# Attention gated by a feed-forward layer: one transpose for both query tiles of a short-reach head

## The chip, the cores and the metric

The kernel runs on one core of one Trainium2 chip. The metric is device time in microseconds (us), taken as the median of several executions. One execution was also recorded by the profiler.

## The reference

The input x has 1024 rows of 512 numbers. After a layer normalisation, two branches are computed from it and joined:

```
xn = layernorm(x)
s  = attention(xn)        # 32 query heads, 8 key/value heads, head size 128
g  = silu(ffn(xn))        # 4-bit weights with scales and zeros, 1792 wide
out = x + s * g
```

The attention is causal with ALiBi, and q and k are normalised per head:

```
scores = q @ k.T / sqrt(128)
bias   = slope[head] * (key - query)  if key <= query else -1e30
attn   = softmax(scores + bias)       # over the keys
s      = concat(attn @ v) @ Wo.T
slope[head] = 0.8409 ** (head + 1)
```

The slopes are steep for the first heads, so that distant keys get weights that vanish. The queries and keys decide whether that holds; the kernel compares this at run time and has a second path without the shortcut.

## The kernel before

**Stages.** The feed-forward branch comes first, then the projections to q, k and v (12 of them, each over 8 row tiles of 128), then the attention with its output projection. The first attention steps are already laid between the tiles of the last projection.

**Units and steps.** The queries are cut into 4 blocks of 256 (`qb` = 0 to 3), each of two query tiles of 128 (`qt` = 0, 1). A unit `u` is one head in one block: `g` is the key/value head, `hh` the head among its 4, so head = 4g + hh. There are 128 units, hence 256 steps `n`, one for each (u, qt). For g = 0 the blocks come in the order 3, 2, 1, 0, for the next ones 2, 3, 0, 1; the 4 heads of a block follow each other. A hand-written order puts the work of several units into each step:

- `scores` at step n: three matmuls for each 512 columns (high and low half of fp16 pairs) into one of two PSUM buffers `s`.
- `biased` and `exponentials` one step later: DVE adds the bias and takes the row's least value (L1073), ACT exponentiates (L1079) into `pf`.
- `split_hi` three steps later: ACT writes the high half of p as fp16 into `p16` (L1098). `split_lo` four steps later: DVE writes the low half beside it (L1106), and SP issues the DMA that transposes the pair of halves from `p16` into `pT` (L1114).
- `values` nine and ten steps later (`AV_LAG`): PE multiplies the transposed p with `vT` into PSUM `o`. Half of the key tiles go into each of the two steps. Key tiles that both query tiles see are one matmul of 256 columns; a tile at either edge of the band has 128 columns.
- `heads_hi`, `heads_lo`, `out_proj` (tile `m`) and `accumulate` follow.

**Reach.** `REACH[head]` is the number of key tiles that a query tile looks back over, its own included: 2 for heads 0 to 2, 3 for heads 3 to 6, 4 for heads 7 to 9, 5 for head 10, 6 for head 11, and 8 (all) from head 12 on. `lowest(u, qt)` is the first key tile of a query tile. Where the reach binds, the two query tiles of a unit see equally many key tiles, the second one tile later than the first.

**Buffers.** `p16` is a ring of 5 slots of 16 blocks of 128x128 fp16 each (`P16_BUFS`). A query tile takes one slot, however little of it it uses. Only in block qb = 0 do both query tiles share a slot: there one DMA transposes both (L1109), with 8 blocks, of which POOL sets some to zero (L1094). `pT` comes from two rings of two slots each, named `wide` and `pT`, taken by turns; it lies as (key tile, half, query), so that the two query tiles of a key tile are 256 neighbouring columns:

```
pT[u] = rings["wide" if u % 4 < 2 else "pT"].take(F16, NT, 2, QB)
sp.dma_start_transpose(
    pT[u][:, k0 : k0 + nk, :, qt * P : qt * P + P]..., h16...)
```

**Queues.** All DMAs are issued by SP in program order: the transposes of p, and between them the loads of keys (L981), values (L985), queries (L993) and of Wo (`load_wo`, L1020, tile `wl`). In a step the loads of keys, values and queries come ahead of `split_lo`; those of Wo end the step.

Of the kernel before, what the change touches and what calls it, by code (L numbers as in the profile page):

```python
# [13 lines left out]
F16 = mybir.dt.float16  # L14
# [8 lines left out]
P = 128  # L23
# [8 lines left out]
NT = S // P  # L32
# [4 lines left out]
NQT = QB // P  # L37
# [76 lines left out]
def attention_gated_by_ffn_kernel(ctx, tc, x, gu_w, gu_z, gu_s, dn_w, dn_z, dn_s, wq, wkv, wo, qnw, knw, out):  # L114
    nc = tc.nc
    ve, se, ge, te, sp = nc.vector, nc.scalar, nc.gpsimd, nc.tensor, nc.sync
# [4 lines left out]
    rings = {}  # L121
# [4 lines left out]
    def ps2():  # L126
        return rings["s"].take(F32, 2, 512)

    def ps1(tag):
        return rings[tag].take(F32, 512)  # L130
# [22 lines left out]
    def mm3(ps, lhs, rhs, first, last):  # L153
        (lh, ll), (rh, rl) = lhs, rhs
        te.matmul(ps, lhsT=lh, rhs=rh, start=first, stop=False)  # L155
        te.matmul(ps, lhsT=lh, rhs=rl, start=False, stop=False)  # L156
        te.matmul(ps, lhsT=ll, rhs=rh, start=False, stop=last)  # L157
# [697 lines left out]
    for it in range(NI):  # L855
        for tb in range(2):
# [14 lines left out]
            for i in range(4):  # L871
                c = slice(i * P, i * P + P)
# [102 lines left out]
    units = [(g, qb, hh) for g, qbs in blocks for hh in range(NH) for qb in qbs]  # L975
    kT, vT, qT, woh, wol = {}, {}, {}, {}, {}
    trel, pT, oT, wor = {}, {}, {}, {}
# [64 lines left out]
    s_ps, pf, rows16, p16, av_ps, op_ps = {}, {}, {}, {}, {}, {}  # L1042

    def lowest(u, qt):

        g, qb, hh = units[u]
        return max(0, NQT * qb + qt + 1 - REACH[g * NH + hh]) if near[0] else 0

    def scores(u, qt):
        g, qb, hh = units[u]  # L1050
        k0 = lowest(u, qt)
        w = (NQT * qb + qt + 1 - k0) * P
        ps = ps2().rearrange("p a c -> p (a c)")
        q = qT[g, qb][:, qt]
        for c0 in range(0, w, 512):
            c1 = min(w, c0 + 512)
            kt = kT[g][:, k0 + c0 // P : k0 + c1 // P]
            mm3(ps[:, c0:c1], (q[:, 0, hh, :], q[:, 1, hh, :]), (kt[:, :, 0, :], kt[:, :, 1, :]), True, True)
        s_ps[u, qt] = ps[:, :w]
# [22 lines left out]
    def split_hi(u, qt):  # L1082
        least, total, inverse, scale = rows16[u]
        if qt == 0:
            ve.reciprocal(inverse, total)
            se.activation(scale, inverse, AF.Copy, scale=P_SCALE)
        nk = pf[u, qt].shape[1]
        if units[u][1]:
            p16[u, qt] = rings["p16"].take(F16, NT, 2, P)[:, :nk]
        elif qt == 0:  # L1090

            both = rings["p16"].take(F16, NT, 2, P)
            both = both.rearrange("p t a k -> p (t a k)")[:, : 4 * NQT * P].rearrange("p (t a i k) -> p t a i k", t=2, a=2, i=NQT)
            ge.memset(both[:, 1, :, 0, :], 0.0)  # L1094
            for i in range(NQT):
                p16[u, i] = both[:, : i + 1, :, i, :]
            p16[u] = both
        se.activation(p16[u, qt][:, :, 0, :], pf[u, qt], AF.Copy, scale=scale[:, qt : qt + 1])  # L1098

    def split_lo(u, qt):  # L1100
        p, h16 = pf.pop((u, qt)), p16.pop((u, qt))
        nk, k0 = p.shape[1], lowest(u, qt)
        if qt == 0:
            pT[u] = rings["wide" if u % 4 < 2 else "pT"].take(F16, NT, 2, QB)
        hi, lo, scale = h16[:, :, 0, :], h16[:, :, 1, :], rows16[u][3][:, qt : qt + 1]
        ve.scalar_tensor_tensor(lo, p, scale, hi, ALU.mult, ALU.subtract)  # L1106
        if u in p16:
            if qt == NQT - 1:
                sp.dma_start_transpose(  # L1109
                    pT[u][:, :NQT].rearrange("p t a (i q) -> p (t a i) q", i=NQT),  # L1110
                    p16.pop(u).rearrange("p t a i k -> p (t a i k)"),
                )
            return
        sp.dma_start_transpose(  # L1114
            pT[u][:, k0 : k0 + nk, :, qt * P : qt * P + P].rearrange("p t a q -> p (t a) q"), h16.rearrange("p t a k -> p (t a k)")
        )

    def values(u, part, between):
        g, qb, hh = units[u]
        if part == 0:  # L1120
            av_ps[u] = ps1("o")[:, :QB]
        ps = av_ps[u]
        k0, k1 = lowest(u, 0), lowest(u, 1)
        kts = [*range(k1, NQT * qb + 2), *range(k0, k1)]
        half = len(kts) // 2
        mine = kts[half:] if part else kts[:half]
        for kt in mine:
            if kt == mine[-1]:
                between()
            c0 = max(0, kt - NQT * qb) * P  # L1130
            c1 = P if kt < k1 else QB
            mm3(
                ps[:, c0:c1],
                (vT[g][:, kt, 0, :], vT[g][:, kt, 1, :]),
                (pT[u][:, kt, 0, c0:c1], pT[u][:, kt, 1, c0:c1]),
                kt == kts[0],
                kt == kts[-1],
            )
# [87 lines left out]
    def early_tile(c):  # L1226

        if c % 2 == 0:
            scores(*at(c // 2))
        for stage, lag in ((biased, 1), (exponentials, 2), (split_hi, 5), (split_lo, 6)):  # L1230
            if (c - lag) >= 0 and (c - lag) % 2 == 0:
                advance(stage, (c - lag) // 2)
# [8 lines left out]
    def step(n):  # L1241
        nonlocal last_ps
        if n < nn:
            u, qt = order[n]
            g, qb, hh = units[u]
            for due in q_at.get(n, ()):
                if due[0] < HKV - 1:
                    load_queries(*due)
            for t, due in LAST_QUERIES.items():
                if due == n:  # L1250
                    last_queries(t)
            if g + 1 < HKV:
                if n % (NB * BS) == KEYS_STEP:
                    relative(g + 1)
                    load_keys(g + 1)
                elif n % (NB * BS) == VALUES_STEP:
                    load_values(g + 1)
            scores(u, qt)
# [6 lines left out]
        for stage, lag in ((biased, 1), (exponentials, 1), (split_hi, NQT + 1), (split_lo, NQT + 2)):  # L1265
            advance(stage, n - lag)
            if stage is biased and ended is not None and units[ended][:2] != final:
                heads_lo(ended)
# [15 lines left out]
        if at(n - AV_LAG):  # L1284
            values(*at(n - AV_LAG), project)
        else:
            project()
# [60 lines left out]
    def everything():  # L1348

        if at(BRANCH - 1 - AV_LAG)[1] == 0:  # L1350
            values(at(BRANCH - 1 - AV_LAG)[0], 1, lambda: None)
        near[0], clock[0] = False, NT * len(projections) - NT
        for c in (kT, vT, qT, woh, wol, pT, oT, wor, s_ps, pf, rows16, p16, av_ps, op_ps):
            c.clear()
        for stage in stages:
            stages[stage] = 0
        relative(0)
        load_keys(0)
        for qb in blocks[0][1]:
            load_queries(0, qb)  # L1360
        load_values(0)
        for n in range(nn + AV_LAG + 1):
            step(n)
# [71 lines left out]
```

## Time and profile before

| | |
|---|---|
| median of 3 runs | 1003.09 us (1000.63 to 1004.23) |
| the profiled execution: time, span | 998.27 us, 996.5 us |
| PE busy | 945.7 us (95%) |
| DVE, ACT, POOL busy | 845.1 (85%), 762.0 (76%), 424.0 us (43%) |
| mean granted TensorE clock | 0.994 |
| DMA queue q1, share of 16 engines | 85.5% |
| transposes of p (L1114 and L1109) | 224 |
| attention steps | from about 442 us to the end |

PE is the TensorE's matmuls, DVE the VectorE, ACT the ScalarE, POOL the GpSimd, SP the SyncE. The line numbers are those of the kernel before. A number in square brackets after an instruction in a timeline is the idle time of its engine just before it, with what ended it. In a table of windows each line gives the stretch, its length, and then the busy time of each engine with its number of instructions. For a DMA issue, the view by line gives the shortest, median and longest time that SP spent on the issue, and in a line of its own the time from the issue to the landing.

### The profile page before, as it was taken

The page shows a single profiled execution, that of the slowest core. Times are in us where ns is not written, and L with a number is a line of the kernel's source. Part 1 is how long each engine was busy: PE and PEld are TensorE (multiplying, and loading weights), DVE is VectorE, ACT ScalarE, POOL GpSimd, SP SyncE. Part 2 cuts the span into 40 slices and gives each one's busy share as a digit, 9 for nine tenths or more (in the row PEclk, how much of TensorE's full clock was granted, in tenths as well). Part 3 has the DMA queues.
Part 4 walks back from the last instruction along what each step waited for, and adds up shares of the span by engine and source line. Part 5 has one row for each costly group of instructions (what it writes and reads, how often), then busy time and mean ns, then how long its engine had stood idle before and what let it go on. Part 6 is the DMA issues. An engine that isn't in the chain of part 4 may idle for free.

```text
span 996.5 us, 17926 instructions
## 1 busy us (share of the span) xinstructions
PE 945.7 (95%) x5595; PEld 550.7 (55%) x5595; DVE 845.1 (85%) x1769; ACT 762.0 (76%) x2161; POOL 424.0 (43%) x437
## 2 busy tenths in 40 slices
PE   7899999999999999999789999999999999989995
PEld 5344467864444444444556565675676666655562
DVE  7898998826988888886789989989989989979985
ACT  5777755678878778788878887878878978867861
POOL 1578864314666565656344231232222313234332
PEclk9999999999999999999999999999999999999999
DMA  7033249734798998997898998998999999999994
GB/s 241 27 118 125 97 125 301 266 127 122 170 255 221 220 259 197 249 256 211 167 205 178 207 209 177 232 203 181 233 202 177 224 191 203 195 231 206 212 207 115
DMA packets 413545, 192.79 MB, mean 193 GB/s; under 512 B 360003, under 2 KB 370559, under 8 KB 413439
## 3 DMA queue, kind: packets, MB, share of 16 engines
q1 hardware_dynamic: 413438, 191.55, 85.5%
q8 instruction: 46, 0.75, 0.3%
q14 instruction: 61, 0.49, 0.2%
HBM read 76.27 MB, written 27.27 MB: 104 GB/s over the span
## 4 chain that ended last, share of the span: by engine, by line
PE 73%; DVE 10%; DMA 8%; ACT 4%; issue 4%; POOL 1%; SPq 0%; DVEq 0%; POOLq 0%; ACTq 0%
PE o L155 8%; PE o L157 8%; PE o L156 8%; PE m L156 8%; PE m L157 8%; PE m L155 8%; PE gu_ps L334 6%; DMA wide<-p 4%; PE s L157 4%; PE s L155 4%; PE s L156 4%; DMA pT<-p 2%; DVE p L1106 2%; PE dn_ps L155 1%; PE dn_ps L157 1%
## 5 line engine op out<-in xcount | busy, mean ns | idle before, releaser
L1106 DVE SCALAR_TENSOR_TENSOR p<-pf,row,p 128x256 f16<-128x256 f32 (+7 forms) x256 | 204.1, 797 | 18.2 <-ACT p L1098 16.0
L1073 DVE CUSTOM_DVE_ANT_0 pf<-s,trel,cs 128x256 f32<-128x256 f32 (+7 forms) x256 | 185.8, 726 | 27.0 <-PE s L157 26.2
L1098 ACT ACTIVATE p<-pf,row 128x256 f16<-128x256 f32 (+7 forms) x256 | 179.3, 701 | 11.4 <-DMA wide<-p 3.2
L1079 ACT ACTIVATE pf<-pf,row 128x384 f32<-128x384 f32 (+7 forms) x160 | 123.2, 770 | 22.2 <-DVE row L1073 20.4
L155 PE MATMUL s<-kT,qT 128*128 128x512 f16 (+3 forms) x344 | 110.1, 320 | 4.5 <-DVE leasts L1073 2.7
L156 PE MATMUL s<-kT,qT 128*128 128x512 f16 (+3 forms) x344 | 110.2, 320 | 0.0
L157 PE MATMUL s<-kT,qT 128*128 128x512 f16 (+3 forms) x344 | 109.0, 320 | 0.0
L724 POOL TENSOR_TENSOR f<-f,inv 128x512 f32<-128x512 f32 (+1 forms) x96 | 99.4, 1056 | 1.3
L1023 POOL TENSOR_SCALAR wl<-wl,rvs 128x512 f32<-128x512 f32 x32 | 52.8, 1651 | 100.2 <-DMA wl<-in_wo 96.5
L1142 ACT ACTIVATE wh<-o 128x256 f16<-128x256 f32 x128 | 47.6, 372 | 60.8 <-PE o L157 60.5
L157 PE MATMUL m<-v,wh 128*128 128x512 f16 x248 | 94.0, 379 | 0.0
L155 PE MATMUL m<-v,wh 128*128 128x512 f16 x248 | 94.0, 379 | 0.0
L155 PEld LDWEIGHTS <-vT 128*128 128x128 f16 x574 | 56.3, 98 | 64.2 <-issue 11.5
L155 PE MATMUL o<-pT,vT 128*128 128x256 f16 (+1 forms) x292 | 75.4, 259 | 12.9 <-DMA pT<-p 10.1
L155 PE MATMUL o<-wide,vT 128*128 128x256 f16 (+1 forms) x282 | 72.9, 259 | 7.5 <-DMA wide<-p 5.6
L156 PEld LDWEIGHTS <-vT 128*128 128x128 f16 x574 | 56.3, 98 | 36.8
L156 PE MATMUL o<-pT,vT 128*128 128x256 f16 (+1 forms) x292 | 75.3, 258 | 0.0
L157 PE MATMUL o<-pT,vT 128*128 128x256 f16 (+1 forms) x292 | 75.0, 258 | 0.0
L155 PE MATMUL m<-wh,xth 128*128 128x512 f16 x192 | 72.8, 379 | 1.2 <-ACT h L898 1.2
L156 PE MATMUL o<-wide,vT 128*128 128x256 f16 (+1 forms) x282 | 72.9, 259 | 0.0
L157 PE MATMUL m<-wh,xtl 128*128 128x512 f16 x192 | 72.8, 379 | 0.0
L156 PE MATMUL m<-wl,xth 128*128 128x512 f16 x192 | 72.8, 379 | 0.0
(213 smaller groups left out, 2583.4 us busy)
## 6 DMA issues: line engine op xcount, KB each, us to landing
qd<-tr SPq DMA_DIRECT2D x48, 256.0 KB, 3.3
qT<-qd SPq DMA_DIRECT2D x24, 512.0 KB, 4.4
wide<-in_wq SPq DMA_DIRECT2D x32, 256.0 KB, 3.9
wo_sq<-in_wo SPq DMA_DIRECT2D x8, 1024.0 KB, 7.8
wl<-in_wo SPq DMA_DIRECT2D x32, 256.0 KB, 3.3
gui<-in_gu_w SPq DMA_DIRECT2D x13, 512.0 KB, 3.6
wide<-in_wkv SPq DMA_DIRECT2D x16, 256.0 KB, 3.7
vd<-v SPq DMA_DIRECT2D x8, 512.0 KB, 4.1
```

The lines of the kernel that those rows point to most:

```text
L155: te.matmul(ps, lhsT=lh, rhs=rh, start=first, stop=False)
L156: te.matmul(ps, lhsT=lh, rhs=rl, start=False, stop=False)
L157: te.matmul(ps, lhsT=ll, rhs=rh, start=False, stop=last)
L334: te.matmul(banks[j][:, k, :], lhsT=w[:, j, ws], rhs=x[:, j, k * 512 : k * 512 + 512], start=x is xth, stop=x is xtl)
L724: ge.tensor_tensor(f, f, ib, ALU.mult)
L1023: ge.tensor_scalar(wor[g, i], wor[g, i], rvs[:, g : g + 1], None, ALU.mult)
L1073: ve.tensor_tensor_reduce(p, ps, trel[g][:, S - w :], cs[:, hh : hh + 1], 3e38, ALU.add, ALU.min, least[:, c])
L1079: se.activation(p, p, AF.Exp, bias=least[:, c], scale=-1.0, accum_out=total[:, c])
L1098: se.activation(p16[u, qt][:, :, 0, :], pf[u, qt], AF.Copy, scale=scale[:, qt : qt + 1])
L1106: ve.scalar_tensor_tensor(lo, p, scale, hi, ALU.mult, ALU.subtract)
L1142: se.activation(oh, av_ps[u], AF.Copy, scale=1.0 / P_SCALE)
```

## The change

For a unit whose two query tiles see equally many key tiles, at most 4 each (`banded`), both tiles take their pairs of p from one slot of `p16`, one behind the other, and one DMA transposes the whole of it after the second tile's `split_lo`. The transposed pairs lie in `pT` in the order of the blocks in `p16`: all key tiles of the first query tile, then all of the second. So `values` reads the two query tiles of a key tile as two runs of 128 columns at a distance (`transposed_p`). That holds for 27 units: heads 0 to 6 in blocks 1, 2 and 3, and heads 7 to 9 in blocks 2 and 3. All other units stay as they were.

```diff
+    def banded(u):
+
+        k0, k1 = lowest(u, 0), lowest(u, 1)
+        return k1 == k0 + 1 and 2 * (NQT * units[u][1] + 1 - k0) <= NT
+
+    def transposed_p(u, kt, half, c0, c1):
+        if not banded(u):
+            return pT[u][:, kt, half, c0:c1]
+        k0 = lowest(u, 0)
+        nk = NQT * units[u][1] + 1 - k0
+        flat = pT[u].rearrange("p t a q -> p (t a q)")
+        begins = [((i * nk + kt - k0 - i) * 2 + half) * P for i in range(NQT)]
+        if c1 - c0 == P:
+            return flat[:, begins[c0 // P] : begins[c0 // P] + P]
+        first = flat[:, begins[0] : begins[0] + P]
+        return bass.AP(first.tensor, first.offset, [first.ap[0], [begins[1] - begins[0], NQT], [1, P]])
+
...
         nk = pf[u, qt].shape[1]
-        if units[u][1]:
+        if banded(u):
+            if qt == 0:
+                p16[u] = rings["p16"].take(F16, NT, 2, P)[:, : NQT * nk]
+            p16[u, qt] = p16[u][:, qt * nk : (qt + 1) * nk]
+        elif units[u][1]:
             p16[u, qt] = rings["p16"].take(F16, NT, 2, P)[:, :nk]
...
         ve.scalar_tensor_tensor(lo, p, scale, hi, ALU.mult, ALU.subtract)
+        if banded(u):
+            if qt == NQT - 1:
+                pairs = p16.pop(u).rearrange("p t a k -> p (t a k)")
+                columns = pT[u].rearrange("p t a q -> p (t a q)")[:, : pairs.shape[1]].rearrange("p (c q) -> p c q", q=P)
+                sp.dma_start_transpose(columns, pairs)
+            return
...
-                (pT[u][:, kt, 0, c0:c1], pT[u][:, kt, 1, c0:c1]),
+                (transposed_p(u, kt, 0, c0, c1), transposed_p(u, kt, 1, c0, c1)),
```

## The prediction

> **What bounds the kernel now.** Every number below is from one profiled execution: its span is 996.5 us, its own time 998.27 us, and the median of the three runs, 1003.09 us, is 0.5% above that. I work out a difference against that execution and take it off the median. About 0.3% (3 us) is what a measurement of this kernel can tell from no change.
>
> The page first: PE is busy 95% of the span, and the chain that ended last is PE for 73% and DMA for 8%. Nearly all of that DMA share is the transposes of p:
>
> ```profile
> PE 73%; DVE 10%; DMA 8%; ACT 4%; issue 4%; POOL 1%; SPq 0%; DVEq 0%; POOLq 0%; ACTq 0%
> wide<-p SPq DMA_TRANSPOSE x112, 4.1
> pT<-p SPq DMA_TRANSPOSE x112, 4.2
> ```
>
> So there are 224 of them, some 4 us from issue to landing. By the reach rule the change touches only heads 0 to 9, and of their units only those whose two query tiles see the same number of key tiles (2, 3 or 4): 9 + 12 + 6 = 27 of the 128 units, 54 of the 224 transposes. They run between 443 and 592 us. What is at stake is read there, in the table of windows (PE, PEld, DVE, ACT and POOL busy, granted clock, DMA share):
>
> ```profile
> 465.00:485.00 20.00, 14.10 (x104) 9.61 (x103) 13.95 (x46) 17.87 (x65) 8.96 (x7) 0.91 0.80 188
> 485.00:505.00 20.00, 16.70 (x134) 10.82 (x133) 17.45 (x63) 17.28 (x60) 2.67 (x7) 1.00 0.88 185
> 525.00:545.00 20.00, 19.86 (x161) 13.42 (x160) 18.41 (x59) 17.78 (x55) 10.42 (x21) 1.00 0.86 176
> 565.00:585.00 20.00, 18.65 (x134) 11.51 (x133) 18.72 (x43) 17.57 (x42) 6.61 (x4) 1.00 1.10 233
> ```
>
> PE is full in the third window, and idle for 5.9, 3.3 and 1.35 us in the others. PE's timeline names the idle stretches one by one; all five before an `o` matmul stand in front of units that the change touches:
>
> ```profile
> 479.94 0.27 PE L155 MATMUL o<-pT,vT 128*128 128x256 f16 x1 [3.30 <-DMA pT<-p]
> 482.66 0.27 PE L155 MATMUL s<-kT,qT 128*128 128x256 f16 x1 [0.59 <-DVE leasts L1073]
> 491.89 0.27 PE L155 MATMUL o<-pT,vT 128*128 128x256 f16 x1 [1.14 <-DMA pT<-p]
> 504.13 0.27 PE L155 MATMUL o<-pT,vT 128*128 128x256 f16 x1 [1.95 <-DVE inv L135]
> 520.70 0.28 PE L155 MATMUL o<-wide,vT 128*128 128x256 f16 x1 [1.77 <-DVE p L1106]
> 574.52 0.27 PE L155 MATMUL o<-wide,vT 128*128 128x256 f16 x1 [1.35 <-DMA wide<-p]
> ```
>
> The gaps at 504.13 and 520.70 are put down to DVE, but the weight loads just before them waited for `DMA pT<-p` and `DMA wide<-p`: these are transposes too. Sum 9.51 us; this is the whole prize on PE.
>
> **What one transpose costs.** A unit with k key tiles per query tile has 2k blocks of 128x128 per query tile (high and low half), so 4, 6 or 8 blocks now and 8, 12 or 16 afterwards. Three views of the transposes by line: 4 blocks (480 to 485 us), the 32 of qb = 0, which are one DMA of 8 blocks already, and 14 or 16 blocks (646 to 666 us):
>
> ```profile
> L1114 SPq DMA_TRANSPOSE wide<-p x2: 1219/1220/1220, 480.1 to 481.4; - x2
> DMA to landing us min/median/max: 2.4/2.5/2.5
> L1109 SPq DMA_TRANSPOSE wide<-p x16: 1231/1232/3107, 501.5 to 972.1; - x16
> DMA to landing us min/median/max: 3.0/3.4/7.0
> L1114 SPq DMA_TRANSPOSE wide<-p x4: 1526/1924/2558, 646.5 to 653.6; - x4
> DMA to landing us min/median/max: 4.4/4.7/5.9
> ```
>
> SP's issue costs 1.22 us up to 8 blocks and 1.5 to 2.6 at 14 to 16; the landing goes from 2.4 (4 blocks) over 3.0 (8) to 4.4: some 1.8 us fixed and 0.15 us a block. So one DMA in place of two saves SP about 1.2 us with k = 2, 0.95 with k = 3 (12 blocks put at 1.5), 0.55 with k = 4 (16 at 1.9): 9 x 1.2 + 12 x 0.95 + 6 x 0.55 = 25.5 us of issuing. On the other hand the last block lands later after its own issue, by 4, 6 or 8 blocks more in the same DMA: 0.6, 0.9 or 1.2 us, because the first tile's half loses its head start.
>
> **What SP's issuing is worth.** SP issues in order, and the second transpose of a pair queues behind the first:
>
> ```profile
> 494.59 3.35 SPq L1114 DMA_TRANSPOSE pT<-p  x2
> 498.03 0.53 SPq L993 DMA_DIRECT2D qT<-qd  x1
> 498.67 2.64 SPq L1114 DMA_TRANSPOSE pT<-p  x2
> ```
>
> No pause between them: the load of queries at 498.03 goes out only when the pair before it is through, and the next pair (head 3, qb 1) directly behind it. The lag of the second issue behind the end of its split (L1106 on DVE), for the five units with a gap:
> - head 3, qb 3: split ends 473.36, issue 474.82, lag 1.46; less 0.9 for the six blocks: 0.55 gained.
> - head 3, qb 2: 486.88, 487.27, lag 0.39, less than the 0.9. But the query load issued at 485.32 is ahead of it in the rings, and the bytes behind that load are the same in one DMA as in two: 0.
> - head 3, qb 1: 498.22, 499.97, lag 1.75. The load ahead is late for the same reason and moves with it, so the whole lag: 1.75.
> - head 4, qb 2: 513.51, 514.73, lag 1.22, less 0.9: 0.3.
> - head 8, qb 2: 566.10, 568.41, lag 2.31; the key load ahead (565.72) follows SP's queue too. Capped by the gap: 1.35.
>
> Together 3.95 us. Bounds of this term: the full lags, 1.46 + 0.39 + 1.75 + 1.22 + 1.35 = 6.2 us gained; and, if no lag is recovered and the head start is lost, 4 x 0.9 + 1.2 = 4.8 us lost.
>
> **The other parts.** A touched unit takes one slot of the five of `p16`, not two. ACT's split (L1098) now waits four times for a transpose to free a slot: 1.76, 0.70, 0.59 and 0.63 us, each beside one of the PE gaps. I expect these to go, but PE still waits for its own transpose, so only what followed is gained: the 0.59 at 482.66 and 0.17 at 485.82, where DVE was late behind ACT: 0.75 us, bounds 0 and 0.75.
>
> Units without a gap must afford 0.6 to 1.2 us. Between the second landing and PE's first `o` matmul most have about 1 us or more, and their lags (0.2 to 3.9 us, mean 1.3) pay for it. Head 7, qb 3 can't: landing 542.45, PE 542.57, lag 0.37, so 1.2 - 0.37 - 0.12 = 0.7 us lost (bounds 0 and 1.1).
>
> The `o` matmuls over both query tiles now read two runs of 128 columns instead of one of 256. The scores already read separate runs of 128 (kT holds high and low halves alternately), and their 256-column matmuls start 0.11 us apart (467.67, 467.77, 467.88), the contiguous `o` ones also (468.32, 468.43, 468.54): 0. ACT's and DVE's splits keep their shapes: 0. Loads of Wo that stood between the two transposes now stand ahead of the single one; their 256 KB had to pass before the second anyway: 0. The first transpose's removed wait for DVE had only SP's loads behind it. Of the 25.5 us of issuing itself nothing counts; SP is not on the chain.
>
> The granted clock: after the 1.96 us idle before 471.52 the matmuls of 256 columns stand 0.21 us apart until 474.9, and the first window's mean is 0.91, which is (1 - 0.91) x 20 = 1.8 us lost. The 3.30 us idle before 479.94 was followed by 0.11. I take 0 for a change of this, bounds -1.8 and +1.8.
> The Trainium skill speaks against later landings here (TensorE: Matmul & The Clock Gate, part 1, "What's actually happening"): an idle window of about 3.4 us halves the clock, and windows run freely; the row at 471.52 dipped after less. By it a wait of 3.30 + 0.9 us would cost one more dip.
> Destination layout: 8 blocks landed in 3.0 us at best with L1109's unbroken destination, and the strided ones of k = 4 also in 3.0 (at 615.98): 0.
> The Trainium skill (DMA: Bandwidth & Descriptors, "Latency and other measured facts") gives transposes 261 GB/s non-contiguous, 350 to 400 contiguous; as an estimate, 12 blocks (393 KB) would land 0.45 us sooner, and the sum would gain 2 us more at the five gaps.
>
> Sum: 3.95 + 0.75 - 0.7 = 4.0 us. The profiled execution would take 994.3 us, the span 992.5, the median 1003.09 - 4.0 = 999.1 us.
>
> **Rivals.**
> - Full lag, chance 0.15: SP's queue is all that delays these landings, 6.2 + 0.75 = 6.9 us, 996.2. For it: issues without a pause. Against: the rings are full as well (DMA share 1.10 from 565 to 585).
> - Nothing, 0.27: landings are set by the bytes queued behind loads, and those don't change; 0.75 from ACT against 0.7 from head 7: 1003.1. For it: unit head 3, qb 2, and SP's lag there. That the change does little because it touches only 27 units, and PE waits for transposes after 600 us too, belongs here.
> - Slower, 0.25: the lost head start. SP's lag was mostly a shadow of full rings and doesn't come back, so the five gaps grow by 4.8 us, head 7, qb 3 by 1.1, head 5, qb 2 (slack 0.5 against 0.9) by 0.4 and head 0, qb 2 by 0.2: 6.5 us, 1009.6. It decides wherever the added blocks times 0.15 us exceed lag plus slack.
>
> **How the numbers follow.** The forecast, 999.1, has 0.33 and a range of its own from 997 to 1002. Range: the runs before lie within 1.8 us of their middle, so 996.2 less 2 gives 994; upwards it takes in no change and half the slower case, 1007. Faster by over 0.3% (below 1000.1): all of the full lag and 0.8 of the forecast, 0.42. Within: 0.2 of the forecast, 0.85 of nothing, some of the slower case, 0.33. Slower: 0.25.
>
> **What would show it.** Right: 197 transposes of p; issues of 1.23 us (k = 2) and 1.4 to 2.6 (k = 3, 4); landings of 3.0 to 3.4, 3.6 to 4.5 and 4.2 to 4.7 us; no ACT wait at L1098 for a slot before 575 us; PE's five gaps down to about 5.5 us. Wrong: gaps that keep their size (bytes decide), new PE gaps before `o` of heads 4 to 9 or a second clock dip (head start), `o` matmuls more than 0.11 us apart (the strided read has a price).

## The result and the profile after

The changed kernel takes 1003.74 us (median of 12 runs, 999.74 to 1009.82), beside 1000.41 us for the kernel before in 12 runs (997.60 to 1007.74): a ratio of 1.0039 with a 95% interval of 1.0020 to 1.0057, so 0.4% slower. A second series gave 1.0040 (1.0025 to 1.0054). The prediction had 0.25 for that side. The profiled execution took 1003.23 us, with a span of 1001.3 us and a mean granted clock of 0.992.

The page after: busy times of the engines, the two queues named "instruction" (number, MB, share of 16 engines), and the group of ACT's splits (L1119, formerly L1098) with its busy time, the mean of one, and the idle time before it:

```profile
PE 946.6 (95%) x5595; PEld 548.7 (55%) x5595; DVE 848.5 (85%) x1769; ACT 761.0 (76%) x2161; POOL 425.7 (43%) x437
q8 instruction: 46, 0.75, 0.3%
q14 instruction: 59, 0.48, 0.2%
L1119 ACT ACTIVATE p<-pf,row 128x256 f16<-128x256 f32 (+7 forms) x256 | 179.2, 700 | 5.9 <-DMA pT<-p 0.5
```

The work is the same and so is PE's busy time to 1 us. The `q8` and `q14` lines count 105 transfers by which the engines get their own instructions: 16 KB each on q8, nearly all of 8 KB on q14. Before there were 46 and 61. The prediction says nothing of these two lines; the experiments lead back to them. Of ACT's waits for a transpose only 0.5 and 0.4 us are left.

The merged transposes by line, with shortest, median and longest issue:

```profile
L1132 SPq DMA_TRANSPOSE wide<-p x16: 1232/1447/5172, 450.3 to 587.3; - x16
L1132 SPq DMA_TRANSPOSE pT<-p x11: 1232/1807/3081, 469.2 to 558.9; - x11
DMA to landing us min/median/max: 3.0/4.7/8.6
```

There are 27, so 197 transposes of p in all. The shortest issue is the 1.23 us that the prediction had, the longest is 5.17 against its 2.6. SP's timeline shows the two longest, of head 0, qb 2 and of head 8, qb 2:

```profile
473.71 3.80 SPq L1132 DMA_TRANSPOSE wide<-p  x1
565.91 5.17 SPq L1132 DMA_TRANSPOSE wide<-p  x1
```

Part of SP's wait has moved into the issue itself. The windows after, over the stretches that the prediction showed and the one between 505 and 525 us (PE, PEld, DVE, ACT and POOL busy, granted clock, DMA share):

```profile
465.00:485.00 20.00, 13.90 (x114) 10.11 (x112) 14.56 (x50) 18.95 (x66) 9.44 (x7) 0.91 0.84 197
485.00:505.00 20.00, 17.85 (x140) 11.21 (x138) 16.97 (x62) 15.74 (x57) 3.80 (x17) 1.00 0.94 176
505.00:525.00 20.00, 17.67 (x107) 9.92 (x105) 16.92 (x46) 14.93 (x44) 9.56 (x5) 0.91 1.08 211
525.00:545.00 20.00, 19.21 (x153) 12.58 (x152) 18.25 (x60) 17.20 (x53) 10.41 (x21) 1.00 0.74 153
565.00:585.00 20.00, 18.34 (x131) 11.19 (x129) 18.57 (x43) 17.07 (x41) 6.97 (x4) 1.00 1.12 226
```

New is the 0.91 in the third line; before, the clock was full there:

```profile
505.00:525.00 20.00, 18.23 (x123) 10.70 (x121) 17.12 (x50) 15.42 (x45) 11.96 (x16) 1.00 0.97 200
```

PE's timeline after, at the first `o` matmul of the five units with a gap before, of head 7, qb 3 (542.26), and of two units late in the kernel that the change doesn't touch (head 19, qb 3 and head 23, qb 3):

```profile
478.64 0.28 PE L155 MATMUL o<-pT,vT 128*128 128x256 f16 x1 [3.59 <-DMA pT<-p]
488.76 0.28 PE L155 MATMUL o<-pT,vT 128*128 128x256 f16 x1 [0.79 <-DVE row L1102]
500.60 0.28 PE L155 MATMUL o<-pT,vT 128*128 128x256 f16 x1 [1.27 <-DMA pT<-p]
517.88 0.33 PE L155 MATMUL o<-wide,vT 128*128 128x256 f16 x1 [2.33 <-DMA wide<-p]
542.26 0.28 PE L155 MATMUL o<-pT,vT 128*128 128x256 f16 x1 [0.63 <-DVE a L738]
574.53 0.28 PE L155 MATMUL o<-wide,vT 128*128 128x256 f16 x1 [1.66 <-DMA wide<-p]
739.23 0.27 PE L155 MATMUL o<-pT,vT 128*128 128x256 f16 x1 [1.18 <-DMA pT<-p]
809.87 0.27 PE L155 MATMUL o<-pT,vT 128*128 128x256 f16 x1 [2.19 <-DMA pT<-p]
```

The five gaps sum to 9.64 us, against 9.51 before. The last two lines stand where before had no gap and one of 0.76 us:

```profile
737.63 0.27 PE L155 MATMUL o<-pT,vT 128*128 128x256 f16 x1
807.52 0.28 PE L155 MATMUL o<-pT,vT 128*128 128x256 f16 x1 [0.76 <-DMA pT<-p]
```

**Where the time went.** I cut the attention at two marks that every kernel has: PE's first `o` matmul of all, and the first one of head 8, qb 0 (606.94 here). Between them lie the touched units, behind them the rest.

| one profiled execution each | touched, us | rest, us | sum | PE's gaps over 0.15 us | stretches at clock 0.5 |
|---|---|---|---|---|---|
| before | 138.4 | 389.7 | 528.1 | 26.5 | 1 |
| before, again | 139.1 | 388.9 | 528.0 | 23.8 | 4 |
| after | 140.6 | 394.4 | 535.0 | 30.0 | 3 |
| after, again | 141.6 | 393.9 | 535.4 | 29.7 | 4 |

(Stretches are counted in units of 3.41 us, between the start of the attention and 990 us.) From the first line to the third: 3.5 us more of gaps, and two more stretches at half clock of 1.7 us each, together the 6.8 us by which the sums differ. (One of the two, at 883 us, the second profile of before has as well, at 881.7. In the second pair the stretches are equally many, and 5.9 us of gaps stand against a difference of 7.4.) The attention starts 1.9 us earlier in the profile of after (466.4 against 468.3), and from kernel to kernel it starts between 466 and 471, which hides some of it in the spans. Two thirds of the difference lie in the rest, in code that the change didn't edit. That was the question for the experiments.

### The profile page after: what moved, and what is told of

Same layout as the page of the kernel before. It is cut to its first block, busy times and chain, and to the rows that moved or that the text cites. A ratio compares the mean times of both kernels' runs of the same rounds, so it can differ in the third digit from the quotient of the medians.

```text
span 1001.3 us, 17820 instructions
## 1 busy us (share of the span) xinstructions
PE 946.6 (95%) x5595; PEld 548.7 (55%) x5595; DVE 848.5 (85%) x1769; ACT 761.0 (76%) x2161; POOL 425.7 (43%) x437
## 5 line engine op out<-in xcount | busy, mean ns | idle before, releaser
L1127 DVE SCALAR_TENSOR_TENSOR p<-pf,row,p 128x256 f16<-128x256 f32 (+7 forms) x256 | 206.3, 806 | 13.7 <-ACT p L1119 11.7
L1119 ACT ACTIVATE p<-pf,row 128x256 f16<-128x256 f32 (+7 forms) x256 | 179.2, 700 | 5.9 <-DMA pT<-p 0.5
L1169 ACT ACTIVATE wh<-o 128x256 f16<-128x256 f32 x128 | 47.4, 370 | 70.1 <-PE o L157 69.9
L155 PE MATMUL o<-wide,vT 128*128 128x256 f16 (+1 forms) x282 | 73.0, 259 | 8.2 <-DMA wide<-p 7.8
L156 PE MATMUL o<-wide,vT 128*128 128x256 f16 (+1 forms) x282 | 73.0, 259 | 0.0
L157 PE MATMUL o<-wide,vT 128*128 128x256 f16 (+1 forms) x282 | 72.9, 259 | 0.0
```

The costliest lines, as they stand in the source:

```text
L1169: se.activation(oh, av_ps[u], AF.Copy, scale=1.0 / P_SCALE)
```

## The experiments

Each ratio is against the kernel before, run on the same chip, with its 95% interval. "Touched" and "rest" are from the one profiled execution of each kernel. Single executions of a kernel lie some 3 us from its median, at times 6, so the ratios decide and the stages only point to a place.

### The kernels themselves once more

The two kernels, unchanged.

> The kernel before itself, run as a changed kernel would be, to show what one profile of it is worth. The stage that the change touches is taken from PE's first o matmul of the first unit to its first o matmul of head 8, block 0 (468.32 to 606.76 us before, so 138.4 us; after the change 140.6 us), and the rest from there to the end (389.7 us before, 394.4 after). If the rest differs by chance alone (theory B: instruction loads and clock dips fall differently in each execution), this second profile moves the rest by 2 us or more and the touched stage by up to 1 us. If the rest depends on the program (theory A: later landings push the clock into dips), both stay within 1 us. The ratio is 1.000 within 0.002 either way.

> The changed kernel again. Theory A (lost head start): the touched stage again lasts 140 to 142 us against 138.4, with five PE gaps in front of the heads that stand behind a load, of 8 to 10 us together, and a dip of the clock inside or just after them. Theory B: the stage comes out between 138 and 141, and the rest anywhere from 389 to 395. Ratio to the kernel before 1.002 to 1.006 by both.

Before: 0.9989 (0.9972 to 1.0005). After: 1.0040 (1.0025 to 1.0054). The loss repeats, and so do the gaps: 2.57, 0, 1.27, 2.34 and 1.69 us at the five units (7.9 us, against 8.9 in the second profile of before), and 1.60 and 1.88 us before the two late units, against 0 and 0.68. So the loss is not an accident of one execution.

### Parts of the change alone

**shared_slot**: one slot of `p16` for both tiles, but two transposes at their own times into the old layout.

```diff
-        if banded(u):
-            if qt == NQT - 1:
-                pairs = p16.pop(u)...
-                sp.dma_start_transpose(columns, pairs)
-            return
-        if u in p16:
+        if banded(u) and qt == NQT - 1:
+            p16.pop(u)
+        if u in p16 and not banded(u):
...                                # and values reads the old layout
```

> The ring of p16 alone: the two tiles of a touched unit share a slot as in the change, but each has its own transpose at its own time into the old layout. Theory A: the head start is kept, so the touched stage lasts 136.5 to 138.5 us; ACT's four waits for a slot (1.76, 0.70, 0.59, 0.63 us) go, the PE gaps stay at about 9.5 us; ratio 0.997 to 1.001. Theory C (the looser ring lets ACT and DVE run ahead at the wrong time and is what costs): ratio 1.002 to 1.006, as with the whole change.

Measured: 1.0007 (0.9989 to 1.0024); touched 138.6, rest 389.3. ACT's waits for a slot are gone here as in after (0.9 us left in all), and the time doesn't move. The looser ring alone is worth nothing that can be measured.

**late_pair**: the shared slot and the old layout, and both transposes issued one behind the other after the second split. This loses the first tile's head start without merging.

```diff
+            pT[u, qt] = h16
             if qt == NQT - 1:
+                for i in range(NQT):
+                    k = lowest(u, i)
+                    sp.dma_start_transpose(pT[u][:, k : k + nk, :, i * P : i * P + P]..., pT.pop((u, i))...)
...                                # in place of the one transpose; values reads the old layout
```

> The head start alone is taken away: shared slot and old layout, and both transposes of a touched unit are issued as two DMAs one behind the other after the second tile's split. The last one is issued 1.2 us after that split at the earliest. Theory A: landings come 0.3 to 0.9 us later than with the merged DMA, PE's gaps grow to 10 to 14 us, the stage lasts 141 to 144 us; ratio 1.004 to 1.009. If the merged DMA or its layout is what costs and not its time (theory C'), this is like the shared slot alone: ratio 0.997 to 1.001.

Measured: 1.0004 (0.9986 to 1.0023); touched 138.5, rest 388.2. The longest of the five gaps, at head 3, qb 3, is 0.75 us shorter than before's 3.30, where 0.9 would have been lost:

```profile
480.17 0.37 PE L155 MATMUL o<-pT,vT 128*128 128x256 f16 x1 [2.55 <-DMA pT<-p]
```

The five gaps sum to 8.9 us. So the lost head start, the mechanism of the slower rival, is refuted: by the interval it costs 2.3 us at most, and not 6.5.

**layout_only**: two slots and two transposes at their own times, but into the new layout, with `values` reading two runs.

```diff
+            w = pairs.shape[1]
+            columns = pT[u]...[:, qt * w : (qt + 1) * w].rearrange("p (c q) -> p c q", q=P)
+            sp.dma_start_transpose(columns, pairs)
...                                # for each tile; p16 has two slots as before
```

> The tile-by-tile layout alone: two transposes per touched unit at their own times and from two slots as before, each into an unbroken stretch of pT, and the values matmuls read two runs of 128 columns. Theory C (the strided read or the new layout costs): the touched stage (first o matmul of the first unit to that of head 8, block 0) lasts 140 to 142 us, as in both profiles of the change (140.6, 141.6); ratio 1.002 to 1.006. Theory P (what costs is where the instruction loads fall once the streams of PE, DVE and SP are 26, 27 and 43 instructions shorter): the streams keep their lengths here, so 138 to 139.5 us for the stage, 388 to 390 for the rest; ratio 0.998 to 1.002.

Measured: 1.0005 (0.9986 to 1.0024); touched 139.8, rest 391.5. The layout and the strided read cost nothing that can be measured, as the prediction had them.

None of the parts loses 0.4%. What is left is the merging itself, or something that only the merging changes.

**only_two**: the whole change, but only for the nine units with two key tiles, where SP gains most by the prediction.

```diff
-        return k1 == k0 + 1 and 2 * (NQT * units[u][1] + 1 - k0) <= NT
+        return k1 == k0 + 1 and 2 * (NQT * units[u][1] + 1 - k0) <= NT and NQT * units[u][1] + 1 - k0 == 2
```

> The change for heads 0 to 2 alone (9 units, 8 blocks in the merged DMA); heads 3 to 9 keep two transposes. By the row of 8 blocks the landing is 0.6 us later, with slack for it. By theory A and by P as far as the stage goes: no gap before unit 23 and no longer one before 16, so the stage takes 137.5 to 139 us. Theory P: the streams are shorter by about a third (PE 8 instructions), so the rest lies somewhere from 388 to 394 us, by where the loads fall; ratio 0.997 to 1.004. If the merging itself costs per unit (theory C'), the stage takes a third of the loss, 139 to 140 us.

Measured: 1.0026 (1.0006 to 1.0047); touched 138.0, rest 393.1. The touched stage is as good as before's, and yet the kernel is slower, behind it. So something seems to reach from the nine units into code hundreds of microseconds later that neither reads nor writes what they made. (The low end of the interval, 1.0006, is close to no loss.)

### The instruction streams

What could reach so far is the length of the programs. Merging takes instructions out: the trace of after has 26 fewer on PE, 27 on DVE and 43 on SP (27 transposes and 16 waits), 5 each on ACT and POOL; that of only_two has 8, 9 and 16 fewer on the first three. An engine's instructions arrive in loads of fixed size: PE's 11,303 of before come in 46 loads of 16 KB, about one for each 250 instructions. With 26 fewer, each later load falls 26 instructions further on in the program, beside other transposes. Counted in units, PE's loads of before lie at 45.6, 48.9, 55.9, 73.2 and 90.9, those of after at 46.1, 49.6, 57.2, 74.2 and 92.1; in shared_slot and late_pair, which keep the length of PE's stream, they lie where they were.

The packet records show what such a load does. In before's trace a load of 16 KB goes out at 476.4 us, and from 476.9 on for 1.5 us hardly a packet of a transpose starts; an 8 KB load at 489.5 is followed by such a stall of 0.8 us, a 16 KB load at 516.9 by one of 1.3 us. Averaged over all 16 KB loads in before's attention, and over the half microseconds with a transpose in flight, 250 to 320 packets of transposes start in a half microsecond up to the load, 60 to 100 in those from 0.5 to 2.0 us after it went out, and then 290 to 380; after an 8 KB load only one half microsecond falls, to 160. In after's trace a 16 KB load goes out at 733.2 and an 8 KB load at 736.1. In the 1.5 us from 733.5 only 114 packets of transposes start, in the half microsecond from 736.5 only 55, and in each of those between, from 735.0 on, 531 to 569. The unit whose transposes are then in flight (issued at 730.15 and 733.09) is head 19, qb 3, with its new gap at 739.23.

So the new theory: the loss is the place of the loads. It can be tested by giving the streams their old lengths back.

**after_padded**: the changed kernel with 26 instructions added on PE, 27 on DVE and 43 on SP, all long before the attention. (The 5 each on ACT and POOL stay missing.)

```diff
-WARM = 40
+WARM = 34
+    for i in range(19):
+        te.matmul(warm[:, :2], lhsT=ones_bf, rhs=ones_bf[:, :2], start=True, stop=True)
...
+    for i in range(16):            # and 11 more in another place
+        ve.memset(spare_column, 0.0)
...
+        if k == 0:
+            for i in range(43):
+                sp.drain(fusable=False)
```

> The changed kernel with its instruction streams made as long again as before, ahead of everything: PE gets 19 tiny matmuls for 6 of its warm-up transposes (26 instructions more), DVE 27 one-column memsets, SP 43 drains before the projections. From about unit 46 on the loads of instructions then stand where they stood in the kernel before. Theory P: the rest (head 8, block 0 to the end) takes 388 to 390.5 us as in the four kernels with the old lengths, not 394; the ratio falls to 0.999 to 1.003. Theory A' (the later stage is slower for what the merged DMAs leave behind, a clock dip or a later start): the rest stays at 393 to 395 and the ratio at 1.002 to 1.006.

Measured: 0.9992 (0.9970 to 1.0014), 997.88 us against 998.30. The whole loss is gone. PE's loads are back at units 45.57, 48.88, 55.87, 73.09 and 90.84, the gap before head 19, qb 3 is 0 again, and the one before head 23, qb 3 is 0.64:

```profile
740.26 0.27 PE L155 MATMUL o<-pT,vT 128*128 128x256 f16 x1
```

In the rest, PE's gaps over 0.15 us are 16.2 us in after and 12.3 here. Of these 3.9 us, 3.8 are three gaps, before head 19, qb 3 (unit 71), head 23, qb 3 (unit 87) and head 24, qb 3 (unit 100): 1.18, 2.19 and 1.07 us there, 0, 0.64 and 0 here.

**before_shifted**: the opposite, without merging: fewer instructions on PE alone, out of its warming up (23 + 4 operations in place of 40). The aim was 26; but the trace has the four as eight matmuls, so PE's stream is 18 shorter.

```diff
-WARM = 40
+WARM = 23
+    for i in range(4):
+        te.matmul(warm, lhsT=ident, rhs=ident.unsqueeze(1).to_broadcast([P, 4, P]), start=True, stop=True)
```

> The kernel before with PE's stream 26 instructions shorter: 27 warm-up operations of the same total length for 40. Nothing else differs, and no transpose is merged. Theory P with PE's loads (16 KB each) as what counts: PE's loads fall 0.5 to 1.2 units later as in the changed kernel, and the rest takes 391 to 395 us with gaps before units 71, 87, 100; ratio 1.001 to 1.005. If the loads of the other engines' streams count, or theory A': 388 to 390.5 us, ratio 0.998 to 1.002.

Measured: 1.0014 (0.9996 to 1.0032); touched 138.7, rest 392.7. The rest lengthens by 3 to 4 us in the profile, but the ratio can't be told from 1. So a shorter stream of PE alone isn't shown to make the loss; nor was it as short as that of after, and its loads went only part of the way (73.8 and 91.3, against 73.2 and 90.9 in before and 74.2 and 92.1 in after). It has a new gap of 1.28 us before head 24, qb 3, with nothing merged. That gap is 0.81 to 1.28 us in all five profiles with a 16 KB load at 99.4 to 99.6 (after, after again, pad_dve and pad_sp below, and this one), and at most 0.36 in all others but layout_only's (1.13, with a load at 99.1).

**pad_pe, pad_dve, pad_sp**: the changed kernel with one of after_padded's three pads each.

> The changed kernel with PE's stream alone made as long again as before (26 instructions, as 19 tiny matmuls for 6 warm-up transposes); DVE's and SP's stay short. The rest was 394.4 and 393.9 us in the change, 390.1 with all three streams restored. If the 16 KB loads of PE are what costs there, the rest falls to 389 to 391 and the ratio to 0.999 to 1.002. If the 8 KB loads of DVE or SP are, PE's gaps before units 71 (1.2 to 1.6) and 87 (about 2) stay, the rest is 392 to 394, ratio 1.002 to 1.005. In between: the gap before unit 100 alone goes, 1 us.

> The changed kernel with DVE's stream alone restored (27 one-column memsets ahead). If DVE's 8 KB loads make the gaps before units 71 and 87, these go and the rest falls by 2 to 3 us to 391 to 392; ratio 1.000 to 1.003. If they don't, the rest stays at 393 to 395; ratio 1.002 to 1.006.

> The changed kernel with SP's stream alone restored (43 drains before the projections). If SP's loads make the gaps before units 71 and 87, the rest falls by 2 to 3 us; ratio 1.000 to 1.003. If they don't, it stays at 393 to 395; ratio 1.002 to 1.006. I give this the least: SP has some 1100 instructions, so 8 or 9 loads in all.

| | ratio | touched, us | rest, us |
|---|---|---|---|
| after, again | 1.0040 (1.0025 to 1.0054) | 141.6 | 393.9 |
| pad_pe | 1.0018 (0.9997 to 1.0039) | 136.2 | 390.9 |
| pad_dve | 1.0033 (1.0015 to 1.0052) | 139.0 | 393.1 |
| pad_sp | 1.0074 (1.0043 to 1.0104) | 141.7 | 395.1 |
| after_padded (all three) | 0.9992 (0.9970 to 1.0014) | 141.0 | 390.1 |

By the middles of the intervals, which overlap, PE's pad takes about half of the loss back, DVE's little, and SP's alone adds some 3 us to it. The interval of pad_sp overlaps that of after, too. The effects don't add up to that of all three. Where loads of two streams fall together counts, as one gap shows over all 19 profiles. Before head 19, qb 3 it is 1.16 to 1.60 us in the four that have a 16 KB load at unit 69.9 to 70.0 and an 8 KB load at 70.4 to 70.5: after, after again, pad_sp and, with nothing merged, before_moved (below). It is 0.39 to 0.53 in three that have only one of the two close to these places (pad_pe, pad_dve and before_dve_sp_moved), and at most 0.34 in the other twelve. From the end of the second split to PE's first `o` matmul that unit takes 8.2 to 8.6 us in the first four and 6.9 in before.

Among the kernels of the table the gap before head 3, qb 3 answers to PE's pad; PE's load near it lies at unit 1.3 with the pad and at 2.3 to 2.45 without. This line is pad_pe's, against 3.59 and 2.57 us in after:

```profile
479.63 0.39 PE L155 MATMUL o<-pT,vT 128*128 128x256 f16 x1 [0.60 <-DMA pT<-p]
```

The load's place isn't all there: before_pe and some_padded (both below) have it at 1.3 too, and gaps of 2.45 and 2.13 us. And in pad_sp the late gap of after stays:

```profile
744.86 0.27 PE L155 MATMUL o<-pT,vT 128*128 128x256 f16 x1 [1.35 <-DMA pT<-p]
```

**before_pe, before_sp, before_all**: the same pads on the kernel before, PE's, SP's, and all three. Without them it could be said that the pads make any kernel faster.

> The kernel before, PE's stream 26 instructions longer ahead of everything, nothing merged. Theory P (place of the instruction loads, whatever is merged): PE's 16 KB load near unit 2.4 moves to about unit 1.3 as in the padded kernels, PE's wait before unit 3 falls from 3.3 to 2 us or less, and the other gaps move; ratio anywhere from 0.995 to 1.003, and the five stages differ from those before by 1 to 3 us. Theory M (the merging costs, the padding merely gives something back): padding is a plain gain, 0.995 to 0.998, the same as it gave the changed kernel (1.004 to 1.0018).

> The kernel before, SP's stream 43 instructions longer, nothing merged. The same padding made the changed kernel slower, from 1.004 to 1.0074. Theory P: a shift of SP's loads alone moves the kernel before as well, by 0.2% or more to either side, most likely slower (1.002 to 1.005). Theory M: no effect without merged transposes, 0.998 to 1.002.

> The kernel before with all three pads (PE 26, DVE 27, SP 43), nothing merged: the control of the padded changed kernel (0.9992), but with loads 26, 27 and 43 instructions beside their old places. Theory P: a different time from the kernel before's, 0.2% or more to either side. Theory M: the pads are a plain gain of 0.4 to 0.5%, 0.995 to 0.997. If it is 1.000 within 0.001, the pads are harmless in themselves, and what they did for the changed kernel is the return of the loads to their old places.

Measured: 0.9992 (0.9978 to 1.0007), 0.9998 (0.9982 to 1.0014) and 0.9991 (0.9972 to 1.0011). Where I had expected shifts of SP's loads, or of all, to move the time by 0.2% or more, none of these moves it measurably: by theory P as I had put it (the places of the loads cost, whatever is merged) that is a miss, and not every place of the loads is bad. The pads are harmless in themselves, then. And merging, compared with the same pads on both sides, is 0.9992 against 0.9991, and with the loads at the same places (after_padded against before) 0.9992: the merging itself neither gains nor loses within some 0.3%. The two profiles speak less plainly (touched 141.0 against 137.3), but that of after_padded was taken in an execution 3.1 us above its median and that of before_all in one 2.6 us below.

**before_moved, before_dve_sp_moved**: the reverse test. Instructions are added to the kernel before until the loads of DVE and SP fall where after has them (one whole 8 KB load of instructions more, less the 27 and 43); before_moved has before_shifted's edit on PE as well, so there PE's stream is again 18 shorter, not 26.

```diff
+        for i in range(9 if it < NI - 1 else 11):     # 101 in all, in the feed-forward branch
+            ve.memset(spare_column, 0.0)
...
+            for i in range(85):
+                sp.drain(fusable=False)
```

> The kernel before with its instruction loads where the changed kernel has them, and nothing merged: PE 26 instructions shorter (27 warm-up operations of the same length for 40), DVE 101 longer (one-column memsets in the feed-forward stage) and SP 85 longer (drains), which is 27 and 43 shorter modulo the 128 instructions of an 8 KB load. Theory P (the places of the loads cost, whatever is merged): the rest takes 392 to 395 us with gaps before units 71, 87 and 100, ratio 1.002 to 1.006. Theory M (the places cost only together with merged transposes): the rest 388.5 to 390.5, ratio 0.998 to 1.002.

> The same without the shift of PE. If DVE's and SP's 8 KB loads make the gaps before units 71 and 87, these come (rest 391 to 393, ratio 1.001 to 1.004); if they need PE's loads beside them, or merged transposes, the rest stays at 388.5 to 390.5 and the ratio at 0.998 to 1.002.

Measured: 1.0113 (1.0089 to 1.0137) and 1.0100 (1.0072 to 1.0128). These ratios can't be used: the pads cost time where they stand, and the attention starts at 474.0 and 476.0 us, 5.7 and 7.7 us later than in the first profile of before. Within the attention, before_moved takes touched 141.0, rest 390.9, sum 531.9, against 528.0, so 3.9 of the 7 us that after takes longer; before_dve_sp_moved takes 527.2. And the gap before head 19, qb 3 is there, with nothing merged in the kernel:

```profile
747.22 0.27 PE L155 MATMUL o<-pT,vT 128*128 128x256 f16 x1 [1.16 <-DMA pT<-p]
```

So the place of the loads makes this gap by itself. That it makes the whole loss in the rest isn't shown by this test: theory P had 392 to 395 us there, and 390.9 and 389.5 are nearer to theory M, by which the places cost only together with merged transposes. PE's loads weren't quite at after's places, though.

### A version with less in it

**some_padded**: the change without units 16, 23 and 32 (head 4, qb 2; head 7, qb 3; head 8, qb 2), three at which PE's gap had grown in the first pair of profiles, and with the streams padded by what is then missing (24, 24 and 38; on PE that is one more than the trace has missing).

```diff
-        return k1 == k0 + 1 and 2 * (NQT * units[u][1] + 1 - k0) <= NT
+        return k1 == k0 + 1 and 2 * (NQT * units[u][1] + 1 - k0) <= NT and u not in (16, 23, 32)
```

> The change without its three units that gain nothing or lose in the stage: head 4, block 2 (PE waits 2.3 to 3.0 us there and the clock dips just after), head 7, block 3 (0.6 to 1.0 us) and head 8, block 2 keep two transposes; 24 units are merged, and the three streams are padded to their old lengths. If the dip at about 520 us comes of the longer wait, it goes, and the stage takes 137.5 to 139 us instead of 141, the rest 388 to 391: ratio 0.995 to 1.000. If the dip follows from the other merged units as well (a longer wait at head 4 in any case), the stage stays at 140 to 141.5 and the ratio at 0.998 to 1.002.

Measured: 0.9988 (0.9967 to 1.0009), 996.79 us against 998.50; touched 135.7, rest 387.2, the shortest attention of all, with no stretch at half clock near 520 us. It can't be told from the kernel before, so no version here is shown to beat it.

## Why the prediction was wrong

**The five gaps (3.95 us gained): the step that failed first.** The prediction took SP's lags behind the splits for time by which the landings would come sooner. The lags did go, from 0.39 to 2.31 us to 0.06 or 0.07 in all five, but the data came no sooner. From the end of the second split to PE's first `o` matmul of the unit, the five units took 6.58, 5.01, 5.92, 7.19 and 8.42 us before, in the order of the prediction, and 7.08, 4.81, 5.50, 7.29 and 8.69 after: 33.1 and 33.4 us (32.9 and 32.5 in the second profiles). What had been a wait ahead of the issue became a wait behind its start: at head 8, qb 2 in the issue itself, of 5.17 us in place of 2.00, at the other four, with issues of 1.49 to 2.17, mostly between the issue and the landing. The gaps went from 9.51 to 9.64 us in the one pair of profiles and from 8.9 to 7.9 in the other, so the term is 0 to 1 us. The reason that the prediction gave for 0 at head 3, qb 2, that the bytes ahead in the rings are the same in one DMA as in two, would fit all five; it is the rival called "nothing", at 0.27, but no run tests it by itself. At head 3, qb 3, the longest of the gaps, a load of instructions seems to have its part: it goes out while the transposes are in flight, and where it doesn't, the gap is 0.60 us in pad_pe and 0.69 in after_padded, though 2.45 in before_pe.

**What the sum didn't contain.** After the edit the streams are shorter by 26, 27 and 43 instructions, and the instruction loads in the attention fall elsewhere. That term is worth +0.5% by the ratios: 1.0040 without the old lengths and 0.9992 with them. No step of the prediction asked what the change does outside its stage, and the case "slower" was tied to a mechanism, the lost head start, that late_pair shows to cost nothing measurable. Slower was right in sign, but by another cause. That 1003.74 us lies within the range of 994 to 1007 is luck as well: the forecast was taken off a median of 1003.09 us, and that of 12 runs is 1000.41. Against it the change is 3.3 us slower, where 4.0 faster was forecast.

**ACT's waits (0.75 us gained).** Right in mechanism: in before's trace PE stood idle for 0.59 us at 482.66 and 0.17 at 485.82, and after has no gap between 478.64 and 486. But shared_slot, which has no such gaps either, shows that it buys no time that can be measured.

**Head 7, qb 3 (0.7 us lost).** It looks right in the first pair and isn't shown: the first profile of before has no gap and after has 0.63 (the split-to-PE time went from 4.40 to 5.19 us), but the second profiles have 0.71 in both (5.27 and 5.26 us), and layout_only has 0.60 with the head start kept.

**The costs put at 0.** Layout and strided read: right (layout_only; matmuls of `o` still 0.11 us apart). The lost head start in units without a gap: nothing seen, as said. SP's own issuing: nothing gained, as said.

**The granted clock (0, bounds of 1.8 us).** After has one more stretch at half clock within the touched units, of 3.41 us from 518.0, right behind the gap of 2.33 us at 517.88; in its second profile it comes at 522.6, after 2.34 us, in after_padded at 520.4, after 3.00, and in pad_sp at 523.0, after 2.15. That is 1.7 us, inside the bound. Of the kernels with nothing merged, none shows one there (gaps of up to 2.2 us, the longest in late_pair), nor pad_dve and some_padded (1.8 and 1.7); but before_shifted and before_moved show one at other touched units, at 493.1 and 581.6. The Trainium skill (TensorE: Matmul & The Clock Gate, part 1, "What's actually happening") has the clock fall after an idle window of about 3.4 us; the stretches of 3.41 us agree with its window, but they follow gaps of 2.3 and 2.7 us here (2.67 before 883.26), while the 3.59 us before 478.64 were followed by none. The row decides: the length of the gap alone doesn't tell.

**Issues and landings.** The fixed and per-block cost were right for the fastest of each size (issues of 1.23, 1.41 and 1.94 us and landings of 3.0, 3.6 and 4.3 for k = 2, 3 and 4), and wrong for the busy ones (up to 5.17 and 8.6).

**What stays open.** Shown are: the loss goes when the streams have their old lengths; it is not in any of the parts that were run alone; the gaps before head 19, qb 3 and, but for one profile, head 24, qb 3 come and go with the place of the loads, merged or not. Not shown is how much each load costs in each place, or why SP's pad alone makes it worse. Whether merged transposes suffer more from a load than split ones stays open too: the unmerged kernels with shifted loads (before_shifted at 1.0014, before_moved's attention) lost less than the merged one, but on PE they were shifted by 18 instructions and not by 26.

## What to carry to other kernels

Here, issuing sooner and in fewer pieces only moved the wait behind the start of the issue. So cost such a change by the time from the producer's end to the landing, and don't count the queue's lag as a gain until something shows that the landing follows it. A change that removes a few dozen instructions also moves the later instruction loads, which here was worth 0.5%, most of it in code that nobody had touched. So before a difference of that size is put down to an edit, pad the streams back to their old lengths, pad the kernel before likewise, and compare again.

## What the runs showed of the hardware

- A load of 16 KB of instructions takes 1.0 us at the median (0.9 to 2.1 in before's attention), and from 0.5 to 2.0 us after it goes out the packets of DMA transposes in flight start at 60 to 100 in a half microsecond in place of 250 to 320; there are 30 such loads in before's attention. The 0.3% and 0.2% on the profile's page hide that.
- 43 drains on SP, long before the attention, gave the changed kernel 1.0074 (1.0043 to 1.0104) in place of 1.0040 (1.0025 to 1.0054), with intervals that overlap, and left the kernel before as it was (0.9998).
- Merging 54 transposes into 27 neither gained nor lost time once that was taken out (0.9992 against 0.9991). The Trainium skill's rates for transposes (DMA: Bandwidth & Descriptors, "Latency and other measured facts"), 261 GB/s "with non-contiguous mid-dim" and 350 to 400 for the contiguous case, would have given layout_only a gain if they hold for the destination, which the page doesn't say; its 1.0005 (0.9986 to 1.0024) shows none, but wouldn't show one of 1 us.
